# Convolution and Haar products take PSUM banks from a second pool while no mixing runs

## The chip, the cores and the metric

The kernel runs on one core of one Trainium2 chip. Its time is the device time of that core in microseconds (us). Before the change it is 2685.84 us, the median of three runs that lay between 2681.97 and 2693.66. The profile is of one execution whose span, from the first instruction to the last, is 2676.0 us.

The core has a matrix engine, TensorE (PE in the profile, with its weight loads as PEld), three engines for elementwise work, VectorE (DVE), ScalarE (ACT) and GpSimd (POOL), and a queue engine, SyncE (SP), that issues the transfers (DMA) here. TensorE writes its products to PSUM, a small memory of eight banks, and VectorE or ScalarE must copy them out before the bank can be used again.

## The reference

The input x has the shape (4, 64, 256, 256): 4 images of 64 channels, 256 by 256, float32. Four layers follow each other.

- Layers 0, 2 and 3 are long convolutions. A small network of sines makes, for each channel, one filter along x and one along y. The 2-D filter is their outer product, and the layer is a causal convolution with it (written with FFTs of twice the size) plus x times a bias per channel.
- Layer 1 takes the 2-D Haar transform of every image, multiplies it by a fixed map v, mixes the 64 channels with a 64x64 matrix, shrinks the result softly by a map tau (sign times what the magnitude exceeds tau by, at least 0), does that for two sets of v, matrix and tau and adds both, transforms back, and adds its own input.

```
k   = einsum('ijk,imk->ijmk', hx, hy)            # layers 0, 2, 3: separable filter
y   = irfft2(rfft2(x) * rfft2(k) / fft_size)[..., :L, :L];  out = y + x * bias
f1  = haar2d(x)                                  # layer 1
f4  = einsum('bchw,oc->bohw', f1 * v[i], conv_w[i])
acc = acc + sign(f4) * relu(abs(f4) - tau[i])    # i = 0, 1
out = haar2d(acc, inverse=True) + x
```

## The kernel before

**Layout.** The kernel works in rounds of M = 4 images (2 of the batch, 2 channels), 64 rounds in two groups of 32. The 256 rows of an image lie as 4 blocks of 64 partitions' worth, so two images share the 128 partitions. Every product is made of 64x64 tiles of TensorE, four of them side by side (two row halves, two column halves; `TILES`).

**Three kinds of work.** `phase_a` is the forward one, layer 0 and the forward Haar transform. In each round: `rows`, a product of the image with the banded matrix of the x filter (tile a1ps, copied to ay by ScalarE, L425); `columns`, the same with the y filter (a2ps, evacuated by VectorE with the bias term into x, L445); the Haar transform along the free axis by sums and differences on GpSimd (`forward_free`, L329 and L331, tiles fw and f); and `product`, the Haar transform along the partitions, on TensorE (a3ps, L293, evacuated by VectorE, L458). The result goes to DRAM (`coef`). `phase_b` is the mixing of one group: a product f4 on TensorE (L575), then multiply, sign, magnitude, subtraction and threshold on VectorE and ScalarE, and adds on GpSimd. It needs four banks of PSUM. `phase_c` is the inverse one: the inverse Haar sums on GpSimd (`inverse_free`, L366, with scalings on ScalarE, L349; their last output is ci), the Haar product c0ps (L293, copied to z, L717), and layers 2 and 3, each with rows (c1r, c2r, copied to ch by ScalarE, L729) and columns (c1c, c2c, evacuated by VectorE, L748).

**The order.** It is written out by hand: each phase is a list of small pieces, and the program runs the pieces of one list, with those of another between them (`beside`). No scheduler reorders anything; each engine works through its own instructions in that order, and semaphores hold it where it needs another's result. There are three stages:

- The first forward stage: 34 rounds of `phase_a` and half of the next, beside the network that makes the filters (`rest`). No mixing runs.
- The middle: the rest of `phase_a` and the first 30 rounds of `phase_c`, beside the mixing of both groups.
- The last inverse stage: the remaining 34 rounds of `phase_c` and a short end, alone (L842). No mixing runs.

In round t the forward stage does a1ps of image set t, a2ps of t-1 and a3ps of t-2. The order within a round is a1ps, a2ps, a3ps, with four, four and two pieces. In the last stage a round is c1r of t, one half of the Haar product of t+1, c2r of t-1, the other half, c1c of t and c2c of t-1. The last round has no Haar product.

**Banks.** Every product of `phase_a` and `phase_c` gets its PSUM from `banks` (L121 to L123): two tiles of 128 x 2 x 256 float32, each the size of one bank, from the pool `acps` of four (L112). So there are two pairs in turn. A convolution pair is filled by two pieces, 32 products; a Haar pair by one piece, 4 products. What copies a finished pair out isn't issued at once: `later` puts it on a list, and `flush` issues the list at the start of the next piece. A product that wants a pair which isn't copied out yet waits.

In the first stage two more banks belong to the network (`mlp_ps`, L156); two pools, `t` and `tps` (L157, L158), are made there and never used. In the middle, four banks belong to the mixing (`bps`). In the last stage only the four of `acps` are in use.

Of the kernel before, what the change touches and what calls it, by code (L numbers as in the profile page):

```python
# [41 lines left out]
F32 = mybir.dt.float32  # L42
AF = mybir.ActivationFunctionType
ALU = mybir.AluOpType
PSUM = bass.MemoryType.PSUM
DRAM = bass.MemoryType.DRAM

P = 128
B, C, N = 4, 64, 256
# [40 lines left out]
def conv_haar_kernel(  # L90
# [17 lines left out]
    def pool(name, bufs, stack=ctx, **kw):  # L108
        return stack.enter_context(tc.tile_pool(name=name, bufs=bufs, reuse_waits="tile", **kw))

    ac = pool("ac", 2)
    acps = pool("acps", 4, space=PSUM)  # L112
# [4 lines left out]
    def blocks(images):  # L117

        return images.rearrange("p (i k) j -> p i k j", i=2)

    def banks(name):  # L121

        return [acps.tile([P, 2, N], F32, tag="ps", name=f"{name}_{r}") for r in range(2)]  # L123

    def load_x(t):
        grp, r = divmod(t, ROUNDS)
# [27 lines left out]
    early = ctx.enter_context(ExitStack())  # L154
    mp = early.enter_context(tc.tile_pool(name="mlp", bufs=1))
    mps = early.enter_context(tc.tile_pool(name="mlp_ps", bufs=2, space=PSUM))  # L156
    tp = pool("t", 1, early)  # L157
    tps = pool("tps", 1, early, space=PSUM)  # L158

    def constant(name, src, shape):  # L160
        t = mp.tile(shape, F32, tag=name, name=f"{name}_sb")
# [239 lines left out]
    def phase_a():  # L401
# [13 lines left out]
        def rows(t, j):  # L415
            s = st[t]
            if j == 0:
                s["y"] = big("t0", f"ay_{t}", 2)
            if j % 2 == 0:
                s["ps"] = banks(f"a1ps{j}_{t}")  # L420
            toeplitz(s["ps"], blocks(s["x"]), filters_x(s["toep"]), j)
            if j % 2:
                for r, ps in enumerate(s["ps"]):
                    y = blocks(s["y"])[:, r, j - 1 : j + 1]
                    later(lambda y=y, ps=ps: nc.scalar.copy(y, ps))  # L425

        def columns(t, j):
            s = st[t]
            if j == 0:
                s["x1"] = big("m0", f"x1_{t}", 2)  # L430
            if j % 2 == 0:
                s["ps2"] = banks(f"a2ps{j}_{t}")
            toeplitz(s["ps2"], blocks(s["y"]), filters_y(s["toep"]), j)
            if j % 2:
                for e, ps in enumerate(s["ps2"]):
                    later(lambda e=e, ps=ps: residual(t, e, j, ps))
            if j == BLOCKS - 1:
                s["fw"] = big("m1", f"fw_{t}", 2)
                s["ops"] = forward_free(s["x1"], s["fw"], f"f{t}_")
# [7 lines left out]
        def product(t, bp):  # L447
            s = st[t]
            if bp == 0:

                s["f"] = big("out", f"f_{t}", 2)
            two = banks(f"a3ps{bp}_{t}")
            fw = blocks(s["fw"])
            haar(two, lambda r, c: fw[half(r), c, 2 * bp : 2 * bp + 2], forward_sb)
            for b, ps in enumerate(two):
                f = s["f"][:, 4 * bp + 2 * b : 4 * bp + 2 * b + 2]
                w = wrow_sb.unsqueeze(1).to_broadcast([P, 2, N])
                later(lambda f=f, ps=ps, w=w: nc.vector.tensor_tensor(f, ps, w, ALU.mult))  # L458
# [347 lines left out]
    def beside(main, side, lead, tail, weights=(1,)):  # L806


        weights = [weights[k % len(weights)] for k in range(len(main))]
        all_of = sum(weights[lead : len(main) - tail])  # L810
        done = 0
        for k, p in enumerate(main):
            p()
            want = len(side) * sum(weights[lead : k + 1]) // max(1, all_of)
            for q in side[done:want]:
                q()
            done = max(done, want)
# [3 lines left out]
    cut_a, cut_c = (ROUNDS + 2) * A_PIECES + BLOCKS + 1, (ROUNDS - 2) * C_PIECES  # L821
    beside(a[:cut_a], rest, 2, 3 * A_PIECES)
    early.close()
    during = ctx.enter_context(ExitStack())
    bp = pool("b", 2, during)
    bps = pool("bps", 2, during, space=PSUM)
# [12 lines left out]
    main = c_first + a_end[:1] + c[:BLOCKS] + c[mid:ends] + a_end[1:] + c[BLOCKS:mid] + c[ends:cut_c]  # L839
    beside(main, phase_b(1), len(c_first) + len(a_end) + 2 * BLOCKS, 0)  # L840
    during.close()
    beside(c[cut_c:], [], 0, 0)  # L842


# [108 lines left out]
```

## Time and profile before

| | us | share of the span |
|---|---|---|
| span | 2676.0 | |
| TensorE matmuls busy (PE) | 2415.2 | 90% |
| weight loads busy (PEld) | 1912.8 | 71% |
| VectorE busy | 1684.8 | 63% |
| ScalarE busy | 1327.5 | 50% |
| GpSimd busy | 1951.0 | 73% |

By stages, with the bounds read from the first weight loads of the rounds (busy us):

| stage | us | PE | PEld | DVE | ACT | POOL | clock |
|---|---|---|---|---|---|---|---|
| first forward, 0 to 474 | 474.00 | 425.72 | 337.51 | 207.66 | 79.64 | 319.25 | 0.98 |
| middle, 474 to 1974.1 | 1500.10 | 1296.64 | 956.67 | 1237.50 | 988.59 | 1264.38 | 0.95 |
| last inverse, 1974.1 to the end | 701.90 | 692.80 | 618.62 | 239.66 | 259.27 | 367.35 | 1.00 |

How to read it. Clock is the TensorE clock that was granted, as a part of full speed. Matmuls are pipelined and the ends that the profile gives them are modelled, so a TensorE that is busy all the time need not be at its peak; the distance between the starts of the same work in two rounds is safer. A float32 product stands in the trace as two matmul records. A line of the timeline has the start, the length, the engine, the line of the kernel, the operation, output and inputs, shapes, and how many instructions are merged in it; in square brackets stands how long the engine was idle before it, and what ended that. "issue" there means that the profile shows nothing that it waited for. Some matmul records can be missing.

### The profile page before, as it was taken

How to read it: one execution, taken by the hardware profiler on the slowest of the kernel's cores; microseconds unless marked ns; L12 is line 12 of the kernel's file. 1: busy time of each engine (PE TensorE's matmuls, PEld its weight loads, DVE VectorE, ACT ScalarE, POOL GpSimd, SP SyncE). 2: the span in 40 equal slices, each digit the busy share in tenths (PEclk: the TensorE clock that was granted, in tenths of full speed). 3: DMA queues.
4: the chain of work that ended last, by engine and by line, in shares of the span. 5: the costliest groups of instructions: out<-in, count | busy, mean ns of one | idle time of the engine just before them, and what ended most of it. 6: DMA issues, size and time to landing. Idle time of an engine off the chain costs nothing.

```text
span 2676.0 us, 120070 instructions
## 1 busy us (share of the span) xinstructions
PE 2415.2 (90%) x53276; PEld 1912.8 (71%) x53276; DVE 1684.8 (63%) x1972; ACT 1327.5 (50%) x2169; POOL 1951.0 (73%) x2422
## 2 busy tenths in 40 slices
PE   6989999777887778868999999999999999999999
PEld 5767778444554445646877787778788888888888
DVE  2454444899999999747878787788753333333333
ACT  1112111466666666426777877777754334334332
POOL 2767778888989889847988887889775655555651
PEclk9999999989999989879999999999999999999999
DMA  5646766698989988646787888888864444444442
GB/s 164 227 165 218 237 221 243 234 353 318 323 320 337 337 314 323 218 158 235 282 309 281 294 302 290 276 293 289 287 199 155 137 152 154 136 149 156 137 133 84
DMA packets 241181, 631.58 MB, mean 236 GB/s; under 512 B 42759, under 2 KB 125352, under 8 KB 224537
## 3 DMA queue, kind: packets, MB, share of 16 engines
q1 hardware_dynamic: 240664, 623.92, 67.0%
q8 instruction: 419, 6.86, 1.0%
q14 instruction: 98, 0.79, 0.1%
HBM read 412.59 MB, written 211.16 MB: 233 GB/s over the span
## 4 chain that ended last, share of the span: by engine, by line
PE 51%; DVE 14%; POOL 11%; DMA 9%; ACT 7%; issue 6%; SPq 2%; DVEq 0%; POOLq 0%; ACTq 0%
PE c2r L281 9%; PE c1c L281 9%; PE c1r L281 7%; PE c2c L281 7%; PE a1ps L281 6%; PE a2ps L281 6%; PE c0ps L293 3%; DVE a L601 3%; PE a3ps L293 3%; POOL f L331 3%; DVE x L590 3%; POOL fw L329 3%; POOL gt L616 2%; PE f L575 2%; DVE m L604 2%
## 5 line engine op out<-in xcount | busy, mean ns | idle before, releaser
L366 POOL TENSOR_TENSOR i<-i,g 128x16 f32<-128x16 f32 x744 | 394.9, 550 | 403.6 <-ACT g L349 386.1
L575 PE MATMUL f<-ft,mix 64*64 64x512 f32 x2048 | 321.7, 638 | 106.2 <-DVE x L590 86.5
L281 PEld LDWEIGHTS a1ps<-tx,x 64*64 64x64 f32 x8192 | 316.3, 139 | 135.2 <-DVE f L458 75.5
L281 PE MATMUL a1ps<-tx,x 64*64 64x192 f32 (+3 forms) x8192 | 360.9, 311 | 37.1 <-DVE f L458 17.9
L281 PEld LDWEIGHTS c2r<-tx,cy 64*64 64x64 f32 x8192 | 310.0, 135 | 87.7 <-ACT ch L729 61.2
L598 ACT ACTIVATE a<-x 128x1024 f32<-128x1024 f32 x256 | 265.0, 1035 | 206.1 <-DVE m L604 205.8
L601 DVE TENSOR_TENSOR a<-a,tau 128x1024 f32<-128x1024 f32 x256 | 314.1, 1227 | 80.3 <-ACT a L598 78.1
L594 ACT ACTIVATE m<-x 128x1024 f32<-128x1024 f32 x256 | 272.2, 1063 | 171.7 <-DVE x L590 108.8
L281 PE MATMUL c2r<-tx,cy 64*64 64x256 f32 (+3 forms) x8192 | 343.3, 303 | 15.2 <-ACT ch L729 11.3
L281 PEld LDWEIGHTS c1c<-ty,ch 64*64 64x64 f32 x8192 | 303.6, 133 | 74.8 <-ACT ch L729 57.7
L590 DVE TENSOR_TENSOR x<-f,v 128x1024 f32<-128x1024 f32 x256 | 311.1, 1215 | 55.9 <-PE f L575 52.6
L281 PEld LDWEIGHTS a2ps<-ty,ay 64*64 64x64 f32 x8192 | 295.9, 135 | 68.4 <-issue 31.1
L281 PE MATMUL a2ps<-ty,ay 64*64 64x128 f32 (+3 forms) x8192 | 326.3, 301 | 15.3 <-ACT ay L425 8.5
L281 PE MATMUL c1c<-ty,ch 64*64 64x128 f32 (+3 forms) x8192 | 332.2, 299 | 8.2 <-ACT ch L729 7.5
L281 PE MATMUL c1r<-tx,z 64*64 64x128 f32 (+3 forms) x8192 | 328.0, 299 | 10.4 <-DMA tx<-filt 6.5
L425 ACT COPY ay<-a1ps 128x512 f32<-128x512 f32 x256 | 137.3, 588 | 401.8 <-PE a1ps L281 401.4
L445 DVE SCALAR_TENSOR_TENSOR x<-x,bias_sb,a2ps 128x512 f32<-128x512 f32 x256 | 179.4, 742 | 249.8 <-POOL f L331 158.9
L281 PEld LDWEIGHTS c1r<-tx,z 64*64 64x64 f32 x8192 | 302.0, 134 | 43.7 <-issue 23.7
L604 DVE SCALAR_TENSOR_TENSOR m<-a,m 128x1024 f32<-128x1024 f32 x256 | 312.7, 1222 | 19.4
L281 PE MATMUL c2c<-ty,ch 64*64 64x256 f32 (+3 forms) x8192 | 318.4, 297 | 3.9 <-issue 3.8
L281 PEld LDWEIGHTS c2c<-ty,ch 64*64 64x64 f32 x8192 | 301.8, 133 | 24.3 <-issue 11.5
L616 POOL TENSOR_TENSOR gt<-gt,m 128x1024 f32<-128x1024 f32 x128 | 303.4, 2370 | 11.9 <-DVE m L604 10.3
(69 smaller groups left out, 3227.0 us busy)
## 6 DMA issues: line engine op xcount, KB each, us to landing
coef<-f SPq DMA_DIRECT2D x256, 256.0 KB, 4.2
ft<-coef SPq DMA_DIRECT2D x256, 256.0 KB, 6.2
v<-in_v SPq DMA_DIRECT2D x128, 512.0 KB, 6.0
tau<-in_tau SPq DMA_DIRECT2D x128, 512.0 KB, 6.5
mixed<-gt SPq DMA_DIRECT2D x256, 256.0 KB, 5.8
g<-mixed SPq DMA_DIRECT2D x256, 256.0 KB, 5.7
x<-in_x SPq DMA_DIRECT2D x63, 1024.0 KB, 5.6
out<-o SPq DMA_DIRECT2D x63, 1024.0 KB, 5.2
```

The costliest lines, as they stand in the source:

```text
L281: nc.tensor.matmul(ps[r][half(c), j % 2, k * ROW :], data[half(r), c, k, bass.ts(j, ROW)], t(r, c)[:, : N - k * ROW], start=k == 0, stop=k ...
L293: nc.tensor.matmul(ps[r][half(c)].rearrange("p h k -> p (h k)"), matrix[half(r)], pairs(r, c).rearrange("p h k -> p (h k)"), start=True, s ...
L366: engine.tensor_tensor(to, s, d, op)
L425: later(lambda y=y, ps=ps: nc.scalar.copy(y, ps))
L445: nc.vector.scalar_tensor_tensor(to, old, bias_sb[:, c : c + 1], ps, ALU.mult, ALU.add)
L575: nc.tensor.matmul(un[u]["f4"][half(q), b, :], mixers[0][half(r), bass.ts(i, C)], st[s]["f"][half(r), b], start=True, stop=True, tile_posi ...
L590: nc.vector.tensor_tensor(un[u]["x"], un[u]["f4"], both(u, "v"), ALU.mult)
L594: nc.scalar.activation(un[u]["m"], un[u]["x"], AF.Sign)
L598: nc.scalar.activation(un[u]["a"], un[u]["x"], AF.Abs)
L601: nc.vector.tensor_tensor(un[u]["a"], un[u]["a"], both(u, "tau"), ALU.subtract)
L604: nc.vector.scalar_tensor_tensor(un[u]["m"], un[u]["a"], 0.0, un[u]["m"], ALU.max, ALU.mult)
L616: nc.gpsimd.tensor_tensor(st[s]["g"], st[s]["g"], m, ALU.add)
```

## The change

`banks` now takes its pairs from a list of pools, `rings`, in turn, and `asked` counts the calls. In the first forward stage the list is `acps`, `acps`, `wide`: the new pool `wide` has two tiles, one pair, so that three pairs go round. It takes the room of two banks that nothing used there; the empty pools `t` and `tps` go. When the first stage ends, the list is set back to `acps` alone, for the middle. When the mixing has ended, a new pool `wide2` of four tiles is opened where the mixing's banks were, and the list is `acps`, `acps`, `wide`, `wide`: four pairs. The purpose is that a product need not wait until an earlier pair is copied out.

```
+    rings = [acps]
+    asked = [0]
+
     def banks(name):
 
-        return [acps.tile([P, 2, N], F32, tag="ps", name=f"{name}_{r}") for r in range(2)]
+        ring = rings[asked[0] % len(rings)]
+        asked[0] += 1
+        return [ring.tile([P, 2, N], F32, tag="ps", name=f"{name}_{r}") for r in range(2)]
...
     mps = early.enter_context(tc.tile_pool(name="mlp_ps", bufs=2, space=PSUM))
-    tp = pool("t", 1, early)
-    tps = pool("tps", 1, early, space=PSUM)
+    rings += [acps, pool("wide", 2, early, space=PSUM)]
...
     beside(a[:cut_a], rest, 2, 3 * A_PIECES)
     early.close()
+    rings[:] = [acps]
     during = ctx.enter_context(ExitStack())
...
     during.close()
+    wide = pool("wide2", 4, space=PSUM)
+    rings[:] = [acps, acps, wide, wide]
     beside(c[cut_c:], [], 0, 0)
```

## The prediction

> **What bounds the kernel now.** I read first the table of busy time by stretches. The pools change in two stages only: the first forward stage (0 to about 474 us, no mixing yet) and the last inverse stage (about 1974 us to the end). Columns: stretch, length, then busy us and instructions of TensorE matmuls, weight loads, VectorE, ScalarE, GpSimd, then clock, DMA share, GB/s.
>
> ```profile
> 402.00:469.00 67.00, 66.24 (x1585) 54.14 (x1581) 27.42 (x42) 12.89 (x24) 54.20 (x95) 1.00 0.70 243
> 2300.00:2400.00 100.00, 100.00 (x2627) 88.92 (x2620) 35.02 (x50) 38.49 (x85) 56.31 (x81) 1.00 0.46 147
> ```
>
> A TensorE that is 100% busy seems to leave nothing to win. But matmul ends are modelled, so I look at what the weight loads waited for, in the last stage and in the forward one (us in total, times, longest).
>
> ```profile
> PEld c2r L281 <- ACT ch L729: 29.5, 64, 0.7
> PEld c1c L281 <- ACT ch L729: 25.9, 57, 0.6
> ...
> PEld a3ps L293 <- DVE x L445: 41.2, 66, 2.9
> PEld a1ps L281 <- DVE f L458: 34.9, 66, 8.7
> ```
>
> The matmuls c2r don't read the ch that these copies write (c1c reads an older one), and a3ps doesn't read x (GpSimd stands between). These are waits for a PSUM bank to be emptied. Now the order of time. Last stage, one round at c0ps, then its final, Haar-free round:
>
> ```profile
> 2306.13 0.20 PEld L293 LDWEIGHTS c0ps<-ci,inverse_sb 64*64 64x64 f32 x4
> 2306.58 1.07 ACT L729 COPY ch<-c1r 128x512 f32<-128x512 f32 x2 [0.90 <-PE c1r L281]
> 2307.22 0.20 PEld L281 LDWEIGHTS c2r<-tx,cy 64*64 64x64 f32 x4 [0.63 <-ACT ch L729]
> 2307.70 4.55 PEld L281 LDWEIGHTS c2r<-tx,cy 64*64 64x64 f32 x123 [0.29 <-ACT ch L729]
> ...
> 2648.22 0.20 PEld L281 LDWEIGHTS c2r<-tx,cy 64*64 64x64 f32 x4
> 2652.58 0.20 PEld L281 LDWEIGHTS c1c<-ty,ch 64*64 64x64 f32 x4
> ```
>
> A Haar product c0ps fills its two banks in under 1 us, too short for two copies of the pair before it, which c2r wants back. Where no Haar product comes between, a group of 64 products runs from 2648.22 to 2652.58: 4.36 to 4.37 us, in all five intervals of the final round. That is TensorE's own pace.
>
> A quiet forward round:
>
> ```profile
> 327.98 0.19 PEld L281 LDWEIGHTS a2ps<-ty,ay 64*64 64x64 f32 x4
> 332.50 0.21 POOL L331 TENSOR_TENSOR fw<-f 128x8 f32<-128x8 f32 x1
> 332.76 0.21 PEld L293 LDWEIGHTS a3ps<-fw,forward_sb 64*64 64x64 f32 x8
> 332.80 1.41 DVE L445 SCALAR_TENSOR_TENSOR x<-x,bias_sb,a2ps 128x512 f32<-128x512 f32 x2 [0.72 <-PE a2ps L281]
> 333.60 0.22 PEld L293 LDWEIGHTS a3ps<-fw,forward_sb 64*64 64x64 f32 x4 [0.63 <-DVE x L445]
> ```
>
> a3ps starts 0.05 us after GpSimd's last piece of fw (332.50+0.21), not at 327.98+4.37 = 332.35. So this stage has two bounds close together: bank waits, and the GpSimd Haar chain.
>
> **What the Trainium skill says.** "PSUM — Partial Sum Buffer", Specifications (TRN2): eight banks of 2 KiB, 512 fp32, per partition. A tile of banks() is 2x256 fp32, one bank; four serve as two pairs now. The forward stage leaves two unused beside the network's two, the last stage four: the new pools fit. "Trainium Kernel Development and Optimization", Best Practices: consistent bubbles can mean that PSUM ran out; the trace agrees, with 0.63 and 0.29 us at the same spot of nearly every round. "TensorE: Matmul & The Clock Gate", Part 2, Step-by-step: weight loads are pulled ahead of matmuls in flight. So a waiting load isn't all lost time, and I price by distances between starts, not by the wait table. The same page, Part 1: a long idle halves the clock (the trace agrees: after 7.84 us idle at 170 us a group took 7.34 us), and one or two busy cores never trip the peak-current limiter; the final round's full pace at 0.99 clock is all that the trace has on that.
>
> **The change part by part.** No arithmetic is added and no engine gets another instruction. The empty pools t and tps that go held no tiles: nothing. Only the pair that each product takes moves.
>
> *Last stage, steady rounds.* Ten pairs a round: c1r two, c0ps one, c2r two, c0ps one, c1c two, c2c two. With two pairs, a product waits for the copies of the second pair before it; with four, for the fourth before it. The shortest run of three pairs between is a c0ps and two pairs of 2.18 us, over 5 us, against 1.07 to 1.41 us for two copies. All bank waits go. What then stands behind? c1c needs c1r's copies, with c0ps and c2r between; c2c needs c2r's, with a c0ps and c1c between; c1r needs z, with c1c and c2c between. ScalarE and VectorE are under 39% busy, GpSimd 56%, DMA 46%. So TensorE's own pace stays: four groups of 4.37 and two Haar products. One Haar product is 4x512 = 2048 columns, a group 64 products of 160 columns on average = 10,240 columns in 4.37 us; by columns that is 0.87 us. The dearer end is the mixing product of the same 2048 columns, 0.91 us from its start to the next in the middle stage (494.27 to 495.18). New round: 17.48 + 1.74 to 1.82 = 19.22 to 19.30 us. Now it is 20.08 (weight loads of c1r from 2603.68 to 2623.77). So 0.78 to 0.86 a round; rounds 32 to 62 are 31: 24 to 27, taken 25.5. Round 31 took 19.92 and gives 0.6. The wait table's 55.4 us would say twice that; half of it was loads waiting ahead of time.
>
> *Last stage, its first round* (weight loads at 1974.10 to 1999.35, 25.25 us). ScalarE stands 12.17 us in its queue before a scaling whose input is still in DMA, and c1r's copies stand behind it. c0ps waits 2.41 us for them, and then c2r runs at the slow clock: c1r's group plus wait 7.24 instead of 4.37, c2r's 6.00 instead of 4.37. With a free pair c0ps needs only ci, which GpSimd finished at 1977.2. Saved 2.87 + 1.63 = 4.5; between 0.8 (if something else holds it) and 4.5 I take 4. Last stage: 30.
>
> *Forward stage.* Six pairs a round: a1ps two, a2ps two, a3ps two. With three pairs, the second a3ps waits for the first a2ps pair, long empty, and a1ps for the second a2ps pair instead of an a3ps pair behind it in VectorE's queue. Quiet round now: a1ps to a2ps 4.70, a2ps to a3ps 4.78, both a3ps 2.10: 11.57. Without bank waits a1ps takes 4.37 and both a3ps 1.75 to 1.82. But the GpSimd loop stays: from the start of a2ps, 4.82 to its second evacuation, 1.41 for that, 0.07 to GpSimd's start, 10.0 of GpSimd (322.71 to 332.71), 0.05: the a3ps of the NEXT round can't start before 16.36 us after this a2ps. Then 1.75 to 1.82 and 4.37 to the second next a2ps: 22.48 to 22.55 for two rounds, 11.24 to 11.28 each. A quiet round gains 0.3, not the 1.05 that TensorE would allow (4.37+4.37+1.78 = 10.52).
> Rounds in which TensorE idles for other reasons (some 15 of the 34 have 0.2 to 2.5 us of "issue" idle) give GpSimd time to catch up and gain more. I took the measured starts of all 34 rounds, kept every such delay and VectorE's network blocks (the 8.7 us wait at 170 us loses only some 2, since the third pair carries one more half group), and stepped them through the conditions "a3ps not before a2ps + 4.37, nor before the earlier a2ps + 16.36" and "a1ps after both a3ps". With today's bank waits the stepping ends at 487.7, measured 485.9; without them 18 to 20 us earlier. Ends: 34 x 0.3 = 10 if every round were quiet, 32 if GpSimd never held. I take 18.
>
> *Middle stage.* Same two pairs, same order: nothing. The mixing's banks lie where the third pair and the network's were; the first mixing product comes twelve pieces later, when those have long been copied out.
>
> Sum: 2685.84 − 30 − 18 = 2638 us.
>
> **The rivals.** (a) The GpSimd chain holds less than I think, and forward rounds reach 10.5: 32 instead of 18, so 2624. For: POOL is busy only 54.20 of 67. Against: a3ps starting 0.05 us after fw in quiet rounds. (b) The forward gain is eaten whole, by the GpSimd loop and by TensorE's "issue" idles coming back elsewhere: 2656. For: quiet rounds already start a3ps with fw. (c) In the last stage a new wait takes the place of the old (copies behind scalings in ScalarE's queue): if half of the stage's gain stays, with the forward 18, 2653; if none, 2668. Against: copies have three pairs of slack. (d) Slower: TensorE fed without gaps gets a lower clock. At 0.92, which stretches of the middle have, 19.26/0.92 = 20.9 a round, 0.85 more than now over 31 rounds is +26, with the forward −18: 2694. For: only the last 26 us of the trace show gap-free feeding. Against: low clocks in this trace go with idle TensorE.
>
> **How the numbers follow.** Forecast (both stages as worked out) 0.60; (a) 0.12; (b) 0.14; (c) 0.10; (d) 0.04. The likeliest is 2638. The range from 2622 to 2660 takes in (a), (b), the milder half of (c) and the bounds of the sizes (38 us saved if every forward round were quiet and Haar products dear, 10 + 28; 62 with the forward stage free of GpSimd). Faster by over 0.5% (below 2672.4): forecast, (a), (b) and most of (c), 0.93; same 0.04, from (c) and a mild (d); slower 0.03.
>
> **What would show it.** In the last stage, weight loads of c2r and c1c no longer wait on ACT ch, and c1r to c1r is 19.2 to 19.3. In its first round c0ps no longer waits for ScalarE. In the forward stage the waits a3ps on x and a1ps on f go, quiet rounds last 11.2 to 11.3, and a3ps still starts right behind GpSimd's fw; a start free of it speaks for (a). The middle stage keeps its length of about 1500 us. Wrong would make it: a stage-wide lower clock, or other waits of the same size at the same places.

## The result

The changed kernel takes 2619.2 us (median of four runs, 2613.91 to 2622.7) against 2687.8 (four runs, 2681.97 to 2693.66). The ratio is 0.9743, 95% interval 0.9723 to 0.9764: 2.6% faster. Forecast were 2638 us, range 2622 to 2660. The direction and both mechanisms came out; the gain is larger than forecast, and the time lies just below the range. The profiled execution of the changed kernel has a span of 2620.6 us.

First the table by stretches, for the changed kernel. Columns as before: stretch, length, busy us and instructions of TensorE matmuls, weight loads, VectorE, ScalarE, GpSimd, then clock, DMA share, GB/s.

```profile
402.00:441.00 39.00, 36.88 (x920) 29.60 (x912) 19.16 (x29) 6.44 (x12) 31.32 (x59) 1.00 0.70 240
2250.00:2350.00 100.00, 99.43 (x2707) 93.97 (x2703) 35.73 (x51) 40.24 (x90) 57.92 (x83) 1.00 0.48 151
```

In the last stage TensorE was "100% busy" before and is 99.43% busy now. What rose is the number of instructions in 100 us, from 2627 to 2707 matmul records: 3% more work in the same time. The clock stayed at 1.00. (The code of the changed kernel is some lines longer: L281 is now L285, L293 is L297, L331 is L335, L445 is L449, L729 is L733.)

Now the last stage, one round, weight loads alone (start and length in us, engine, line, operation), the lines between the groups' starts left out.

```profile
2096.43 0.21 PEld L297 LDWEIGHTS c0ps<-ci,inverse_sb 64*64 64x64 f32 x4
...
2096.86 4.81 PEld L285 LDWEIGHTS c1c<-ty,ch 64*64 64x64 f32 x124
...
2101.66 0.21 PEld L285 LDWEIGHTS c2c<-ty,ch 64*64 64x64 f32 x4
...
2106.03 0.21 PEld L285 LDWEIGHTS c1r<-tx,z 64*64 64x64 f32 x4
...
2110.39 0.21 PEld L297 LDWEIGHTS c0ps<-ci,inverse_sb 64*64 64x64 f32 x4
...
2115.62 0.15 PEld L297 LDWEIGHTS c0ps<-ci,inverse_sb 64*64 64x64 f32 x2
```

From one c0ps to the second next is 2096.43 to 2115.62 = 19.19 us, a whole round (20.08 before). c2c to c1r is 4.37. From 2096.43 to c2c, so a Haar product and a group, is 5.23; less 4.37 that leaves 0.86 us for a Haar product of four times 512 columns. And what the weight loads of c2r and c1c waited for, in 1980 to 2610 us (us in total, times, longest; there are only these two):

```profile
PEld c2r L285 <- issue: 8.1, 36, 0.7
PEld c1c L285 <- issue: 5.4, 28, 0.2
```

The waits on ScalarE's copies are gone. "issue" here is the load's own pace; the rounds above have no room for more.

The first round of that stage, weight loads alone, before (lines left out as above):

```profile
1974.10 0.20 PEld L281 LDWEIGHTS c1r<-tx,z 64*64 64x64 f32 x4
...
1981.34 0.22 PEld L293 LDWEIGHTS c0ps<-ci,inverse_sb 64*64 64x64 f32 x4 [2.52 <-POOL i L366]
...
1982.39 0.29 PEld L281 LDWEIGHTS c2r<-tx,cy 64*64 64x64 f32 x4 [0.44 <-ACT ch L729]
...
1988.39 0.20 PEld L293 LDWEIGHTS c0ps<-ci,inverse_sb 64*64 64x64 f32 x4
...
1996.07 3.37 PEld L281 LDWEIGHTS c2c<-ty,ch 64*64 64x64 f32 x98 [0.78 <-issue]
```

and after:

```profile
1950.36 0.20 PEld L285 LDWEIGHTS c1r<-tx,z 64*64 64x64 f32 x4
...
1954.72 0.19 PEld L297 LDWEIGHTS c0ps<-ci,inverse_sb 64*64 64x64 f32 x4
...
1958.41 2.04 PEld L285 LDWEIGHTS c2r<-tx,cy 64*64 64x64 f32 x56 [0.29 <-ACT ch L733]
...
1969.92 0.20 PEld L285 LDWEIGHTS c1r<-tx,z 64*64 64x64 f32 x4
```

c0ps starts 4.36 us after c1r, instead of 7.24, and waits for no copy; c2r still shows one short wait for a copy, 0.29 us. The round takes 19.56 us instead of 25.25. The granted clock over c2r was 0.76 before (1981 to 1988 us) and is 1.00 now (1955 to 1960.5 us).

The forward stage, two quiet rounds, all engines, with most lines left out:

```profile
303.24 0.20 POOL L335 TENSOR_TENSOR fw<-f 128x8 f32<-128x8 f32 x1
...
303.50 0.21 PEld L297 LDWEIGHTS a3ps<-fw,forward_sb 64*64 64x64 f32 x8 [0.34 <-POOL fw L335]
...
304.84 0.15 PEld L285 LDWEIGHTS a1ps<-tx,x 64*64 64x64 f32 x4 [0.28 <-DVE x L449]
...
309.57 4.47 PEld L285 LDWEIGHTS a2ps<-ty,ay 64*64 64x64 f32 x128
```

and the next starts, weight loads alone:

```profile
314.87 0.21 PEld L297 LDWEIGHTS a3ps<-fw,forward_sb 64*64 64x64 f32 x8 [0.82 <-POOL fw L335]
...
325.75 0.21 PEld L297 LDWEIGHTS a3ps<-fw,forward_sb 64*64 64x64 f32 x8 [0.34 <-POOL fw L335]
```

The two a3ps now take 1.34 us (303.50 to 304.84) instead of 2.10, and do not wait for VectorE. (The a1ps behind them takes 4.73; together that is 6.07 us, forecast 6.12 to 6.19.) They start 0.06 us after GpSimd's last piece of fw (303.24 + 0.20). Rounds alternate, 11.37 (303.50 to 314.87) and 10.88 (314.87 to 325.75), mean 11.12. The second profile alternates between 10.45 and 11.81 at places, 11.13 in the mean. Over two rounds that is the loop of the prediction: from a2ps at 309.57 to the a3ps of the next round at 325.75 are 16.18 us, forecast 16.36. What the weight loads of the stage waited for, in 60 to 441 us of the changed kernel, some lines left out:

```profile
PEld a3ps L297 <- POOL fw L335: 17.4, 20, 2.7
...
PEld a1ps L285 <- DVE x L449: 7.6, 20, 2.6
PEld a1ps L285 <- DVE f L462: 7.0, 2, 6.6
...
PEld a3ps L297 <- DVE x L449: 2.8, 10, 0.3
```

The waits of a3ps for VectorE fell from 41.2 to 2.8 us. Those of a1ps for a3ps's evacuation fell from 34.9 to 7.0, nearly all of it one block of the filter network. A smaller new wait, 7.6 us of a1ps for a2ps's evacuation, is there as well, so a few bank waits are left.

By stages, all from the starts of the same work. Each stage is read from every profile that has the same pairs in it: two pairs in the forward stage from the kernel before, a second run of it and the change of the last stage alone; three pairs from the changed kernel, a second run of it, the change of the forward stage alone and a run with three pairs in the last stage; and in the same way for the last stage.

| stretch | two pairs there | three or four pairs there | saved |
|---|---|---|---|
| forward, 32 rounds from the a1ps of image set 3 | 412.4, 416.8, 408.9 | 379.5, 380.4, 378.2, 379.4 | 33.3 |
| last stage, its first 33 rounds | 669.8, 669.5, 669.7 | 638.1, 637.2, 638.4 | 31.7 |

The middle, from the end of that forward stretch to the start of the last stage, took 1502.9, 1503.3 and 1505.6 us where the forward stage had two pairs, and 1509.2, 1512.4, 1511.8 and 1506.4 where it had three. Its own order and pairs are the same in all. Two further runs with two pairs, in which only the load of x is split (below), have 1509.9 and 1511.2 there. So the third pair as such does not make the difference; its cause is open.

### The profile page after: what moved, and what is told of

It is laid out like the page before. It is cut to its first block, busy times and chain, and to the rows that moved or that the text cites. A ratio compares the mean times of both kernels' runs of the same rounds, so it can differ in the third digit from the quotient of the medians.

```text
span 2620.6 us, 120068 instructions
## 1 busy us (share of the span) xinstructions
PE 2357.1 (90%) x53276; PEld 1908.0 (73%) x53276; DVE 1686.6 (64%) x1972; ACT 1325.3 (51%) x2169; POOL 1951.1 (74%) x2422
## 3 DMA queue, kind: packets, MB, share of 16 engines
q8 instruction: 419, 6.86, 1.1%
## 4 chain that ended last, share of the span: by engine, by line
PE 42%; DVE 12%; DMA 10%; POOL 9%; ACT 6%; issue 5%; SPq 2%; DVEq 0%; ACTq 0%; POOLq 0%
PE c1c L285 9%; PE c2r L285 9%; PE c2c L285 8%; PE c1r L285 8%; PE c0ps L297 3%; DVE a L605 3%; PE f L579 3%; DVE x L594 3%; POOL f L335 2%; POOL fw L333 2%; DVE m L608 2%; DMA ft<-coef 2%; ACT a L602 2%; DMA mixed<-gt 2%; DVE x L449 2%
## 5 line engine op out<-in xcount | busy, mean ns | idle before, releaser
L285 PEld LDWEIGHTS a1ps<-tx,x 64*64 64x64 f32 x8192 | 303.4, 140 | 132.9 <-DVE f L462 47.8
L285 PE MATMUL a1ps<-tx,x 64*64 64x192 f32 (+3 forms) x8192 | 341.5, 309 | 29.3 <-DVE f L462 15.3
L285 PEld LDWEIGHTS c2r<-tx,cy 64*64 64x64 f32 x8192 | 319.1, 135 | 62.2 <-ACT ch L733 28.8
L285 PEld LDWEIGHTS c1c<-ty,ch 64*64 64x64 f32 x8192 | 311.3, 133 | 53.4 <-ACT ch L733 29.8
L285 PE MATMUL c2r<-tx,cy 64*64 64x64 f32 (+3 forms) x8192 | 330.9, 301 | 13.6 <-ACT ch L733 10.9
L285 PE MATMUL c1r<-tx,z 64*64 64x128 f32 (+3 forms) x8192 | 326.7, 299 | 13.1 <-DMA tx<-filt 6.7
L285 PEld LDWEIGHTS c1r<-tx,z 64*64 64x64 f32 x8192 | 303.0, 134 | 46.4 <-issue 26.4
L285 PEld LDWEIGHTS a2ps<-ty,ay 64*64 64x64 f32 x8192 | 281.4, 135 | 74.1 <-issue 27.2
L285 PE MATMUL a2ps<-ty,ay 64*64 64x256 f32 (+3 forms) x8192 | 319.1, 301 | 12.5 <-ACT ay L429 9.1
L285 PE MATMUL c1c<-ty,ch 64*64 64x192 f32 (+3 forms) x8192 | 321.1, 298 | 7.0 <-ACT ch L733 6.2
L285 PE MATMUL c2c<-ty,ch 64*64 64x192 f32 (+3 forms) x8192 | 316.4, 297 | 3.6 <-issue 3.6
L285 PEld LDWEIGHTS c2c<-ty,ch 64*64 64x64 f32 x8192 | 303.2, 133 | 22.4 <-issue 10.9
L449 DVE SCALAR_TENSOR_TENSOR x<-x,bias_sb,a2ps 128x512 f32<-128x512 f32 x256 | 179.4, 743 | 214.1 <-POOL f L335 132.1
```

Of the source, the lines that this page charges most:

```text
L285: nc.tensor.matmul(ps[r][half(c), j % 2, k * ROW :], data[half(r), c, k, bass.ts(j, ROW)], t(r, c)[:, : N - k * ROW], start=k == 0, stop=k ...
L449: nc.vector.scalar_tensor_tensor(to, old, bias_sb[:, c : c + 1], ps, ALU.mult, ALU.add)
```

## The experiments

My theory after the result: both gains are bank waits, and they add; in the last stage TensorE's own pace is left, in the forward stage GpSimd's loop over two rounds. What the prediction missed lies in the forward stage and is not GpSimd but TensorE's "issue" idles. The rivals: GpSimd holds less than I thought, or the two stages help each other.

**Each kernel again.** The kernel before and the changed one, unedited.

> The kernel before, once more: how much a stage's length varies from run to run. The forward stage (a1ps of its second round to a1ps of its last, 58.75 to 471.19 us, 412.4 us) gave up 16.7 us in the first profile to idles of TensorE called issue, and that of the changed kernel only some 3. If those idles come by chance, another amount is seen here, and the forward stage is shorter or longer by about the difference. If they belong to this order of work with two pairs, again 14 to 19 us and 412 us within 3. The timed ratio is 1.000 within 0.004 either way.

> The changed kernel, once more. Quiet forward rounds alternate between 10.88 and 11.37 us again, the last stage has 19.19 us a round. If the few issue idles (some 3 us in the forward stage) came by chance, they are more here and the forward stage is up to 10 us longer than the 379.5 us of the first profile (61.72 to 441.21); if three pairs take them away, again below 6 us. Time 2614 to 2623.

Measured: before against itself 1.0005 (0.9992 to 1.0019); changed 2621.3 us, ratio 0.977 (0.975 to 0.9789). The result repeats. The "issue" idles of the kernel before were there again, 18.9 us, but its 32 forward rounds took 416.8 us, further from 412 than the 3 us expected.

**One stage alone.** Forward only: the changed kernel without

```
-    wide = pool("wide2", 4, space=PSUM)
-    rings[:] = [acps, acps, wide, wide]
```

> Three pairs in the forward stage alone, two in the last. By the prediction's terms 18 us less than before (ratio 0.9933); by the profile of the changed kernel 30 to 37 less (ratio 0.986 to 0.989). The last stage as before: 20.08 us a round.

Last stage only: the changed kernel without

```
-    rings += [acps, pool("wide", 2, early, space=PSUM)]
```

> Four pairs in the last stage alone, two in the forward one. By the prediction and by the profile of the changed kernel 30 to 32 us less than before (ratio 0.988 to 0.989), with 19.19 us a round. If the two parts don't add (the sum of both single gains differs from 68 us by more than 8), something that both share was missed, in the middle stage most likely.

Measured: forward only 2649.24 us, ratio 0.9878 (0.9852 to 0.9903), 33.1 us less than the 2682.29 of before beside it. Last stage only 2648.55, ratio 0.9876 (0.9853 to 0.9899), 33.7 less. Together 66.8; the whole change gave 61.0 beside them (2682.29 − 2621.3) and 68.6 in the first comparison. So the parts add, within what the kernel before varies by. The last stage gives 33.7, a little over the forecast of 30; the forward stage gives 33, not 18.

**Three pairs instead of four in the last stage.**

```
-    wide = pool("wide2", 4, space=PSUM)
-    rings[:] = [acps, acps, wide, wide]
+    wide = pool("wide2", 2, space=PSUM)
+    rings[:] = [acps, acps, wide]
```

> The changed kernel with three pairs in the last stage instead of four. A product then waits for the third pair before it. The shortest two pairs between are a c0ps and one of c1r or c2r, 0.86 + 2.18 us, more than two copies need (1.07 to 1.41). So the round stays 19.19 us and the time within 3 us of the changed kernel. If the fourth pair matters (copies queued behind scalings), the round is 19.3 to 19.8 and the time 4 to 20 us longer.

Measured: 2619.18 us, ratio 0.975 (0.9719 to 0.9781), as with four pairs. Of its 33 rounds 19 take 19.18 us (20 to 23 of them with four pairs); all take 640.9 us together against 637.2 to 638.4. The first of them, 23.5 us instead of 19.3 to 19.6, is more than that difference. In the steady rounds one Haar product and one pair of 2.18 us (half a group) between a pair and its next use already cover the two copies (1.07 to 1.41 us). In these single profiles the fourth pair is worth 2 to 4 us, in the first round; in the timed runs nothing can be seen of it.

**Does GpSimd's loop hold the forward rounds?** In the forward stage, the first difference of the Haar transform is computed twice: one more GpSimd instruction of 1.9 us in each round.

```
+            if half == HALF and int(name[1:-1]) < ROUNDS:
+                nc.gpsimd.tensor_tensor(diffs, even, odd, ALU.subtract)
```

> The changed kernel with the first difference of the Haar chain (1.89 us on GpSimd) done twice in the forward rounds of the first group; the result is the same. If the loop over two rounds bounds the stage (16.17 us from a2ps to the next round's a3ps, then both a3ps and a1ps 6.07), a quiet round takes (16.17 + 1.89 + 6.07) / 2 = 12.07 us, 0.95 more, and the time is 25 to 32 us longer than the changed kernel's. If GpSimd has slack, under 8 us longer.

Measured: 2651.87 us, ratio 0.9872 (0.9844 to 0.99) to the kernel before, so 31 to 33 us more than the changed kernel, all of it in the forward stage (412.1 us for the 32 rounds against 379.4). Weight loads in a run of quiet rounds of it (L337 here is L335 of the changed kernel):

```profile
377.42 0.21 PEld L297 LDWEIGHTS a3ps<-fw,forward_sb 64*64 64x64 f32 x8 [1.40 <-POOL fw L337]
...
389.72 0.21 PEld L297 LDWEIGHTS a3ps<-fw,forward_sb 64*64 64x64 f32 x8 [1.76 <-POOL fw L337]
...
401.66 0.21 PEld L297 LDWEIGHTS a3ps<-fw,forward_sb 64*64 64x64 f32 x8 [1.40 <-POOL fw L337]
```

12.30 and 11.94, mean 12.12: 1.00 us a round more than 11.12, for 1.9 us of GpSimd. That is what a loop over two rounds does: the addition enters it once, so half of it falls on each round. The quiet rounds are GpSimd's; rival (a), which wanted them at 10.5, falls.

**Taking a3ps out of the loop.** On the changed kernel, the Haar product is done some 2.2 us later: between the pairs of the next round's a1ps instead of just before it. So fw has the time of one pair more.

```
+                if j in (1, 2) and 2 < t < ROUNDS + 3:
+                    product(t - 3, j - 1)
...
-                if t > 1:
+                if t > ROUNDS + 1:
                     product(t - 2, j - 2 * BLOCKS)
```

> The changed kernel, and in the forward stage the two Haar products of an image set go a round later in part: between the two pairs of a1ps of the next round, so that GpSimd has 2.18 us (one pair) more for the same work. Nothing else moves. If the GpSimd chain bounds the forward rounds with three pairs, quiet rounds fall from 11.12 to TensorE's own 10.45 to 10.6 us, and the time by 15 to 22 us against the changed kernel (some 2601). If something else on TensorE holds them (bank waits left over, late instructions), the time stays within 4 us of the changed kernel.

Measured: 2608.1 us, ratio 0.9713 (0.9687 to 0.9738), 11 to 13 less than the changed kernel. Quiet rounds reach 10.45, as expected, TensorE's own pace; the 32 rounds take 371.0 us, in the changed kernel 379.4 on average. The gain falls short of the 15 to 22 us expected, because few rounds are quiet. What is left, the longest of the weight loads' waits in 60 to 441 us of this run:

```profile
PEld a1ps L285 <- issue: 20.2, 67, 1.4
PEld a2ps L285 <- DVE f L462: 9.6, 4, 4.5
```

GpSimd is gone from the head of the list (its wait for fw, 17.4 us in the changed kernel, is 1.6 here). Two waits of over 4 us are blocks of the filter network in VectorE's queue, which a3ps's evacuation stands behind. This version beats both kernels.

**What are the "issue" idles?** With two pairs TensorE's matmuls stand idle in the forward stage (60 to 470 us) 16, 18 and 16 times, 16.7, 18.9 and 14.9 us in all, in the three profiles. With three pairs it is 5, 7, 5 and 7 times, 3.3, 3.9, 3.2 and 3.8 us. So about 13.3 us went that the prediction had kept. Matmuls of the convolutions, in the second run of the kernel before:

```profile
268.78 3.28 PE L281 MATMUL a2ps<-ty,ay 64*64 64x256 f32 x86 [0.42 <-issue]
...
292.69 0.21 PE L281 MATMUL a1ps<-tx,x 64*64 64x64 f32 x1 [1.08 <-issue]
...
305.86 0.65 PE L281 MATMUL a1ps<-tx,x 64*64 64x192 f32 x14 [1.86 <-issue]
```

They come in a drifting place of a round. But counted in all of TensorE's instructions (weight loads, matmul records, and the waits that stand between them in its program), every one of the 74 idles in these seven profiles begins at 193 or 194 after a multiple of 256. The list of the DMA queues (packets, MB, share of the engines) has what goes by 256 instructions; in the changed kernel:

```profile
q8 instruction: 419, 6.86, 1.1%
```

6.86 MB in 419 packets are 16.4 KB each. TensorE has 2 x 53,276 instructions and 896 waits: 256 to a packet. The Trainium skill, "Runtime: NRT & Kernel Launch", Instruction fetch mechanics, says that instructions are refilled in 16 KiB blocks of 256, by a DMA queue of the engine's own, and that the cost is mostly hidden. Sizes agree with the trace. "Mostly hidden" doesn't hold in this stage. Number the packets in order, and the k-th belongs to the k-th multiple of 256. It starts at the earliest 101 instructions before this multiple and is missed 193 after it: 294 instructions, an estimate of 5.0 us at full pace (a group of 64 products has 256 records and takes 4.37 us). Every one of the 74 idles ended 1.2 to 1.6 us after its packet had landed, so these are waits for instructions.

With two pairs the packets start 42 to 54 instructions behind the multiple on average (60 to 441 us), 13 to 17 of 62 to 64 more than 90 behind; with three pairs 3 to 9 behind on average. They stand behind data. A load of x is 1 MB and lands 4.8 to 6.3 us after its issue. In the two profiles of the kernel before (60 to 470 us) none of the 135 packets starts in the first 4 us after such an issue, 61 start 4 to 6 us after it, and among these are 32 of the 33 that are more than 90 behind.

If so, cutting the load of x must take the idles away with two pairs too. On the kernel before, x comes in four transfers of 256 KB, one for each of the next round's first four pieces:

```
+        if parts is not None:
+            parts += [(xs[:, k : k + 2], x[grp, r, :, k : k + 2]) for k in range(0, 2 * M, 2)]
+            return xs
...
+            if j < BLOCKS and x_parts:
+                nc.sync.dma_start(*x_parts.pop(0))
...
-                if j == 2 * BLOCKS + 1:
+                if j == 2 * BLOCKS + 1 and t < ROUNDS:
+                    st[t + 2]["x"] = load_x(t + 2, x_parts)
+                elif j == 2 * BLOCKS + 1:
                     load(t + 2)
```

> The kernel before, two pairs, and in the forward stage the image load of 1 MB goes out as four loads of 256 KB, one with each a1ps piece of the next round, instead of at once when a1ps begins. The idles of TensorE called issue begin always after the same count of its instructions (193 within 256), at the end of a fetched packet, and follow a packet that started late. If the fetches are late because they queue behind such a burst of transfers, the idles fall from 15 to 19 us to under 8 and the time by 6 to 12 us against before. If the lateness belongs to the bank waits themselves, the idles stay above 13 us and the time within 4 us of before.

Measured: the idles fell to 4, 2.5 us; the 32 rounds took 403.8 us, 9 less than the mean of two pairs; but the time is 2678.9 us, ratio 0.9983 (0.9972 to 0.9994), only some 5 less, under the 6 to 12 expected. The first two rounds took 29.64 us together and the third 14.30, instead of 23.08 and 12.78 in the first profile of the kernel before. So once more, from the load of round 6 on:

```
-                if j == 2 * BLOCKS + 1 and t < ROUNDS:
+                if j == 2 * BLOCKS + 1 and 3 < t < ROUNDS:
```

> The kernel before, with the load of x split into four transfers of 256 KB, each issued one piece of the work apart, but only from the load of round 6 on, so that the start of the kernel stays as it was. Theory (the 'issue' idles of TensorE are instruction packets that queue behind the 1 MB load): the idles in 60 to 470 us fall from 15 to 19 us to under 5 and the timed gain over the kernel before is 9 to 12 us, ratio 0.9955 to 0.997. Rival (the earlier run of this split gained only some 4 to 6 us because the idles' time goes into other waits): a gain of under 6 us, ratio over 0.9978.

Measured: 2671.34 us beside 2683.28, ratio 0.9956 (0.9943 to 0.997), 12 us less, with idles of 3 times, 1.9 us. The packets start 1 instruction behind on average. That an unsplit load makes TensorE's instructions late is shown, and taking the lateness away this way gains 12 us. What it costs by itself is less sure. In the profile of this run the 32 rounds take 405.1 us, 7.6 less than the mean of two pairs, and TensorE now waits 8.5 us for x in them: the split load has waits of its own.

**Both on the changed kernel.** The Haar product 2.2 us later, as in the run before (not a whole round), and the split load from round 6 on.

> The changed kernel with two further changes: the forward Haar product a whole round later (as in the run late_haar), and the load of x split in four transfers of 256 KB from the load of round 6 on. Theory: late_haar's rounds are held by late instruction packets (5 us) and little else that a split load touches, so 2600 to 2605, ratio 0.968 to 0.970. Rival: the parts land later than the single load did, rounds of 10.45 us then wait for x, and the time is 2608 or more.

Measured: 2632.5 us, ratio 0.9802 (0.9773 to 0.9832), 24 us slower than the later Haar product alone. The rival came out. Idles of "issue" are down to one of 0.8 us, but now the products wait for x (queue engine and weight loads):

```profile
313.75 2.72 SPq L485 DMA_DIRECT2D x<-in_x  x4
...
319.34 0.73 PEld L288 LDWEIGHTS a1ps<-tx,x 64*64 64x64 f32 x16 [1.09 <-DMA x<-in_x]
```

The four parts stand behind the filter loads in SyncE's order and go out from 313.75 to 316.47; the last two land 4.5 and 5.2 us after their issue. TensorE waits for the first parts until 318.09 and for the next until 319.34. In 60 to 440 us weight loads wait 27.8 us for x, the sum of 18 waits, about what was lost. SyncE has little room left: from 200 to 400 us it spends 177 us on issuing, against 165 in the run of the later Haar product and 128 in the kernel before. TensorE's matmuls stand idle for x 22.4 us here, against 8.5 with two pairs and rounds of 11.57 us. That the shorter rounds make the difference is likely, but the split load was not tried with three pairs alone. The theory that this run set out from was itself only half right: of the nine "issue" idles of the later Haar product, 5.0 us, four with 2.4 us neither stand at the count of 193 nor end 1.2 to 1.6 us after a packet; what they wait for is open.

## Why the prediction was right, and where it was not

- **Last stage, steady rounds: right.** 19.18 to 19.19 us (forecast 19.22 to 19.30), the Haar product 0.86 (0.87 to 0.91). Rounds 32 to 62: mean 20.15 before, 19.29 after, 26.6 us against 25.5. No new wait took the old one's place: rival (c) falls. That half of the wait table's 55.4 us would be lost time is right too; 26.6 us came back. The clock stayed at 1.00 in the gap-free stretch: rival (d) falls.
- **Last stage, its ends: right in kind.** The first round gave 5.7 us instead of 4. What was forecast gave 3.8 of it: c1r with the wait behind it 2.9, and c2r 0.9, as it took 5.12 us (6.00 before, not down to 4.37, though the slow clock was gone). The rest was not in the forecast: 1.2 from the two Haar products' own bank waits, and 0.9 from c2c, where an "issue" idle of 0.78 went. Round 31 took 20.56 after and 19.92 before, so it gave nothing here (19.18 in the run of the last stage alone). The two misses, 1.7 too little and 1.2 too much, nearly cancel: all in all 31.7 against 30.
- **Forward stage: the mechanism was right, the size was not, 33 instead of 18.** The loop through GpSimd was there (16.18 us against 16.36; a3ps right behind fw; the doubled instruction moved the round by half of itself). The step that failed is "kept every such delay": the measured "issue" idles of TensorE were carried over into the new schedule as fixed, and they were not a property of the rounds. They fell from some 16.9 to 3.6 us, 13.3 less, because the instruction packets behind them came in time; the split load alone, with two pairs, took as much of them away and gained 12. Taken one for one, which is an estimate, that leaves 33.3 − 13.3 = 20 us for bank waits and loop, against 18. The loop itself was a little shorter than forecast, 11.12 us a quiet round instead of 11.24 to 11.28. Rival (b), which had these idles coming back elsewhere, falls: the opposite happened.
- **The range's low end** was built from the two sizes that I had called uncertain (GpSimd, Haar product), with the idles held fixed. So it stopped at 62 us saved. Rival (a) names nearly the measured time, 2624, for a reason that the runs refute: its 32 us for the forward stage are near the 33 measured by chance.
- **Middle stage: nothing forecast;** some 6 us more in the profiles on average, cause open.

What stays open: why the third pair, without a split load, keeps instruction packets on time. One difference is seen: with two pairs a load of x goes out 0.63 us before the first a1ps (311.08 and 311.71 us in the kernel before), with three 0.07 us before (304.77 and 304.84), so bursts and packets meet at other places of the count. With three pairs 11 to 13 packets of a profile start within 4 us after such a load goes out, with two none or one. That this is the cause was not tried.

## What to carry to other kernels

Where products of unlike length share a ring of banks, count how many pairs lie between a use of a pair and its next, and take the shortest such run against the evacuation: here a third pair was enough and the fourth bought nothing measurable. Price it by distances between starts of the same work, not by the table of waits. Before a delay is carried over into the new schedule as fixed, ask what it hangs on: here the "issue" idles that came at a fixed count of instructions belonged to the instruction stream and the transfers beside it, and went when either was shifted.

## What was not expected of the hardware

- TensorE's instructions come in packets of 16.4 KB, 256 to a packet. Beside 1 MB loads they were late 16 to 18 times in 410 us, up to 2.46 us each, 14.9 to 18.9 us in all; each of these idles ended 1.2 to 1.6 us after the packet had landed.
- The same 1 MB in four parts lifted that (1.9 us left), yet in the kernel with three pairs and the later Haar product, whose quiet rounds take 10.45 us, the parts cost more than they gave: 24 us slower.
- Moving products to another pair of banks, with no transfer added, changed how late the instruction packets were: from 42 to 54 instructions behind on average to 3 to 9.
